# Four graph layers on one core: a reordered softmax, first pairs one step sooner, a bias add in pieces, and a normalisation moved to ScalarE

## Chip, cores and metric

The kernel runs on one core of a Trainium2 chip. Five engines share the core's on-chip memory: PE (TensorE, matrix products), ACT (ScalarE), DVE (VectorE), POOL (GpSimd) and SP (SyncE, which here issues the transfers). The metric is the device time of one execution in microseconds (us), as the median of several runs. Smaller is better.

## What is computed

`x` holds 32 batches of 512 nodes with 128 features, `adj` is a sparse 512 x 512 matrix. Four layers follow each other, each of the form x = x + layer(relu(layernorm(x))). Cut to what matters:

```python
h = relu(layernorm(x))                       # layer 0
A = softmax(where(adj > 0, e[position], -9e15), axis=1)
x = x + (A*I) @ (h @ W0) + (A*(1-I)) @ (h @ W1) + bias

h = relu(layernorm(x))                       # layer 1
x1 = adj^T h;  x2 = 2*adj^T x1 - h
x = x + relu(concat(h, x1, x2, x1, x2) @ Theta1 + bias)

h = relu(layernorm(x))                       # layer 2
f = relu(h @ psi_w + psi_b);  msg = (adj*adj)^T f
x = x + relu(concat(msg, h) @ phi1_w + phi1_b) @ phi2_w + phi2_b

h = relu(layernorm(x))                       # layer 3
S = exp(8*tanh(((h@q) @ (h@k)^T) / sqrt(128) / 8)) * adj
x = x + (S / rowsum(S)) @ h @ v
```

All is in float32. Inputs and output lie in the chip's main memory.

## The kernel before

**Tiling.** The 32 batches are worked on as 16 pairs, q = 0 to 15. A pair's `x` is one tile of 128 partitions x 2 batches x 4 blocks of 128 nodes x 128 features. All 16 pairs stay on chip through the four layers, so `adj` and what is derived from it are made once.

**Names.** `bn` are the layer norm's statistics (L194, VectorE), `sd` the roots (L200, ScalarE), `rs` and `sh` the scale and shift (L203, L205, VectorE). `h` is the normalised tile. It is made by eight ScalarE instructions of 128x128 (L216), which apply scale, shift and relu at once. In layer 3 alone it is made by eight VectorE instructions (L229) and two relus on ScalarE (L231). `hT` is h with features on the partitions. For the pairs 0, 1 and 2 of layer 0 it is made by transposes on the PE and two copies on ScalarE (L248, L251). For the others it goes through VectorE's 32x32 transposes (`hb`, L258) and a bounce through main memory (L262, L265).

**Prep (up to L614).** Inside the `by_source` block the PE, VectorE, ScalarE and GpSimd run in the order of the source. The block builds the softmax matrix `att` from `adj`, with the exponentials in `softmax_rows` (L550) and the division in `scaled_rows` (L560). `transpose_rows` (L400) makes `attT`. The chebyshev matrix `cheb` is made in four pieces (L409), each of four matmuls of 512 columns, an eviction and a correction of the diagonal. The layer norm of pairs 0 and 1 runs between these, as the generators `normal`, `turned` (hT) and `project` (the product with W1, called `g`).

**Matrix products.** Products of a 512 x 512 matrix with a pair are formed from seven half-size products (`products`, L299, in the order of `ORDER`, L296). They need sums of the matrix's quarters (`sum_steps`) and of the pair's (`right_blocks`, `rt`, on GpSimd). Each product's bank is emptied by one instruction: in `mixed` (L323) by ScalarE for two of them and by VectorE for the rest. The banks are named a, c and d (`p_msgT_a` and so on), and c and a are used again by later products.

**The layers.** `layer0(q)` does the seven products with `att`, adds the diagonal part and ends with the statistics for layer 1. `layer1(q)` makes x1T and x2T, and then p_l (L706), y (L709) and the new x (L710). `layer2(q)` makes `feat` (L721 to L724), msgT, adds the bias phi2b to x on GpSimd as one instruction (L730), and then makes h1T (L737) and x (L741). `layer3(q)` makes, for each batch of the pair, p_qkh and p_hv, then four score blocks with tanh and exp (L765 to L770), and then p_av (L777), the division, the add to x and the output transfer (L784).

**Order.** After the prep, generators are called in turn. `waiting` is a list of groups of generators. In every step the next group joins `active`, and each active generator advances by one `yield`. This gives the order in which instructions are emitted. A scheduler then orders each engine's instructions, with the exception of those marked `keep_in_program_order`, and every engine runs its own queue. `layer0_first(q)` makes h, hT and g of a later pair, so that layer 0 finds them ready; `loads(q)` starts the transfers of later pairs; `square()` and `late_sums()` prepare the matrices of later layers.

```python
waiting = [[layer0(q)] for q in range(NQ)]          # L806
for q in range(2, NQ):
    waiting[max(q - 4, 0)].append(first[q])
waiting += [[layer1(q)] for q in range(NQ)]
```

Of the kernel before, what the change touches and what calls it, by code (L numbers as in the profile page):

```python
# [11 lines left out]
AF = mybir.ActivationFunctionType  # L12
# [3 lines left out]
P = 128  # L16
# [8 lines left out]
def kernel(  # L25
# [98 lines left out]
    def spread(w, n):  # L124
        return w[:, None, :].to_broadcast([P, n, D])
# [86 lines left out]
    def normed_steps(q, h):  # L212
        for b in range(2):
            for t in range(NT):
                i = b * NT + t
                nc.scalar.activation(h[:, b, t, :], xt[q][:, b, t, :], AF.Relu,  # L216
                                     bias=shift[q][:, i : i + 1], scale=scale[q][:, i : i + 1])
                yield

    def normed(q, on_act=True):  # L220
        h = normed_tile(q)
        if on_act:
            for _ in normed_steps(q, h):
                pass
            return h
        for b in range(2):
            for t in range(NT):
                i = b * NT + t
                nc.vector.tensor_scalar(h[:, b, t, :], xt[q][:, b, t, :], scale[q][:, i : i + 1],  # L229
                                        shift[q][:, i : i + 1], OP.mult, OP.add)  # L230
            nc.scalar.activation(h[:, b], h[:, b], AF.Relu)  # L231
        return h


# [165 lines left out]
    def transpose_rows(banks, src, t):  # L400

        for j in range(NT):
            nc.tensor.transpose(banks[j][:, blk(t)], src[:, t, blk(j)], ident)
# [156 lines left out]
    def scaled_rows(t, u):  # L560
        nc.vector.reciprocal(total[:, t : t + 1], total[:, t : t + 1])
        nc.scalar.mul(split(att[:, t, :]), crossed(u), total[:, t : t + 1])
        own = split(att[:, t, :])[:, :, t, :]
        d = diag[:, t, :].rearrange("p (b c) -> p b c", c=QR)
        nc.gpsimd.tensor_mul(d, own, ident.rearrange("p (b c) -> p b c", c=QR))
        nc.gpsimd.tensor_sub(own, own, d)
# [8 lines left out]
    pt = [bank(f"p_attT_{j}") for j in range(NT)]  # L575
    us = []
    for t in range(NT):
        if t == NT - 1:
            next(project[0], None)
        us.append(softmax_rows(t))  # L580
        if t == 0:
            next(ln[1], None)
        else:
            scaled_rows(t - 1, us[t - 1])
        for _ in range(3):
            next(normal[1], None)
    scaled_rows(NT - 1, us[-1])
    next(turned[1])
    for t in range(NT):
        transpose_rows(pt, att, t)  # L590
    next(turned[1], None)
    nc.scalar.copy(qk, p[:, :D])
    rights = {0: right_of(0)}
    next(project[1])
    for q in (2, 3):
        next(ln[q])
    for j in range(NT):
        (nc.vector.tensor_copy if j % 2 else nc.scalar.copy)(attT[:, j, :], pt[j])
    next(project[1], None)
    for _ in sum_steps(attT, "att", nc.vector):  # L600
        pass
# [6 lines left out]
    for q in (2, 3):  # L608
        next(ln[q])
        next(ln[q], None)  # L610
    for i in (2, 3):
        for _ in pieces[i]:
            pass
    by_source.__exit__(None, None, None)  # L614


# [96 lines left out]
    def layer2(q):  # L713
        h = normed(q)
        yield
        hT = transposed(h, f"hT2_{q}")
        yield
        yield
        feat = []
        for b in range(2):  # L720
            pf = projected(f"p_feat_{q}_{b}", (at(hT, b), psi))  # L721
            feat.append(late.tile([P, NT, D], F32, tag="y", name=f"feat_{q}_{b}", bufs=2))
            nc.vector.tensor_add(feat[b], pf, spread(psib, NT))
            nc.scalar.activation(feat[b], feat[b], AF.Relu)  # L724
        yield
        right = right_blocks(lambda J, b: feat[b][:, 2 * J : 2 * J + 2, :], f"feat_{q}", [nc.gpsimd] * 4)
        msgT = pair_tile(f"msgT_{q}").rearrange("p (b w) -> p b w", b=2)
        for _ in mixed(f"msgT_{q}", sums["sq"], right, msgT):
            pass
        nc.gpsimd.tensor_add(xt[q], xt[q], phi2b[:, None, None, :].to_broadcast([P, 2, NT, D]))  # L730
        yield
        h1T = pair_tile(f"h1T_{q}").rearrange("p (b w) -> p b w", b=2)
        for b in range(2):
            ph = bank(f"p_phi1_{q}_{b}")
            nc.tensor.matmul(ph, phi1[:, 1, :], hT[:, :, b, :], start=True, stop=False)
            nc.tensor.matmul(ph, phi1[:, 0, :], msgT[:, b], start=False, stop=True)  # L736
            nc.scalar.activation(crossed(h1T[:, b]), split(ph), AF.Relu, bias=phi1b)  # L737
        yield
        for b in range(2):
            po = projected(f"p_l2_{q}_{b}", (columns(h1T[:, b]), phi2))  # L740
            nc.vector.tensor_add(xt[q][:, b], po, xt[q][:, b])  # L741
        ln_stats(q)

    def layer3(q):
        h = normed(q, on_act=False)
        yield
        hT = transposed(h, f"hT3_{q}")
        yield
        yield
        for b in range(2):  # L750
            pp = bank(f"p_qkh_{q}_{b}")
            nc.tensor.matmul(pp, qk, hT[:, :, b, :], start=True, stop=True)  # L752
            both = work.tile([P, 2 * N + 2 * NT], F32, tag="pair", name=f"qkh_hv_{q}_{b}", bufs=5)
            qkh = both[:, :N]
            nc.vector.tensor_copy(crossed(qkh), split(pp))

            pv = projected(f"p_hv_{q}_{b}", (at(hT, b), vw))
            hv = both[:, N : N + NT * (D + 1)].rearrange("p (t f) -> p t f", f=D + 1)
            nc.gpsimd.memset(hv[:, :, D : D + 1], 1.0)
            nc.vector.tensor_copy(hv[:, :, :D], pv)  # L760
            yield
            ex = square_tile(f"ex_{q}_{b}")
            for t in range(NT):
                ps = bank(f"p_score_{q}_{b}_{t}")
                nc.tensor.matmul(ps, hT[:, t, b, :], qkh, start=True, stop=True)  # L765
                nc.scalar.activation(ex[:, t, :], ps, AF.Tanh, scale=1.0 / (8.0 * math.sqrt(D)))  # L766
            for t in range(NT):
                nc.scalar.activation(ex[:, t, :], ex[:, t, :], AF.Exp, scale=8.0)  # L768
                eng = nc.gpsimd if t % 2 else nc.vector
                eng.tensor_mul(ex[:, t, :], ex[:, t, :], adjTx[0][:, t, :])  # L770
            yield
            rsum = stats.tile([P, NT], F32, tag="rsum", name=f"rsum_{q}_{b}", bufs=4)
            for i0 in range(0, NT, 2):
                po = bank(f"p_av_{q}_{b}_{i0}").rearrange("p (i f) -> p i f", i=2)
                for i in range(2):
                    for t in range(NT):
                        nc.tensor.matmul(po[:, i, : D + 1], ex[:, t, blk(i0 + i)], hv[:, t, :],  # L777
                                         start=(t == 0), stop=(t == NT - 1))
                nc.vector.reciprocal(rsum[:, i0 : i0 + 2], po[:, :, D])
                for i in range(2):  # L780
                    xi = xt[q][:, b, i0 + i, :]
                    nc.vector.scalar_tensor_tensor(xi, po[:, i, :D], rsum[:, i0 + i : i0 + i + 1], xi,
                                                   OP.mult, OP.add)
            nc.sync.dma_start(out[2 * q + b].rearrange("(t p) f -> p t f", p=P), xt[q][:, b])  # L784

    adjTx = []

    def square():

        sq = square_tile("sq")  # L790
        load_crossed(sq, adj)
        adjTx.append(square_tile("adjTx"))
        load_crossed(adjTx[0], adjT_d)
        yield
        for i in range(NT):
            s = late.tile([P, N], F32, tag="hs", name=f"sq_{i}", bufs=2)
# [8 lines left out]

    waiting = [[layer0(q)] for q in range(NQ)]  # L806
    next(waiting[0][0])
    for q in range(NQ // 2, NQ):
        waiting[q - NQ // 2].append(loads(q))
    for q in range(2, NQ):  # L810
        waiting[max(q - 4, 0)].append(first[q])
    waiting[3].append(late_sums())
    waiting += [[layer1(q)] for q in range(NQ)]
    waiting[NQ + 6].append(square())
    for layer in (layer2, layer3):
        waiting += [[layer(q)] for q in range(NQ)]
    active = []
    while waiting or active:
        if waiting:
            active += waiting.pop(0)  # L820
        active = [g for g in active if next(g, active) is not active]


# [30 lines left out]
```

## Time and profile before

| what | value |
|---|---|
| median of 3 runs | 998.58 us (997.66 to 998.66) |
| the profiled execution's own time | 1000.32 us |
| its span, first to last instruction | 998.5 us |
| mean granted PE clock | 0.993 |
| last matmul ends | 994.34 us |
| instructions | 16127 |

In the profile a line such as `L216 ACT ... x384 | 154.5, 482` means: the instruction of line 216 ran 384 times on ScalarE, 154.5 us in all, 482 ns each. After the next bar stands the idle time of the engine just before these instructions, and what ended it. A timeline gives start, duration, engine, line, operation, output and inputs; idle time before an instruction stands in brackets with what released it. The stages can be told from the lines that run: the prep up to about 49 us, layer 0 to about 201, layer 1 to about 487, layer 2 to about 717, and layer 3 to the end.

### The profile page before, as it was taken

How to read it: one execution, taken by the hardware profiler on the slowest of the kernel's cores; microseconds unless marked ns; L12 is line 12 of the kernel's file. 1: busy time of each engine (PE TensorE's matmuls, PEld its weight loads, DVE VectorE, ACT ScalarE, POOL GpSimd, SP SyncE). 2: the span in 40 equal slices, each digit the busy share in tenths (PEclk: the TensorE clock that was granted, in tenths of full speed). 3: DMA queues.
4: the chain of work that ended last, by engine and by line, in shares of the span. 5: the costliest groups of instructions: out<-in, count | busy, mean ns of one | idle time of the engine just before them, and what ended most of it. 6: DMA issues, size and time to landing. Idle time of an engine off the chain costs nothing.

```text
span 998.5 us, 16127 instructions
## 1 busy us (share of the span) xinstructions
PE 976.4 (98%) x5918; PEld 809.4 (81%) x5918; DVE 630.4 (63%) x1520; ACT 440.9 (44%) x967; POOL 395.1 (40%) x478
## 2 busy tenths in 40 slices
PE   8999999999999999999899999999999999999997
PEld 4699999989999999998777777777667777767776
DVE  8678787655555655558667888777754444444443
ACT  4863537112322323237566343333464455544452
POOL 2579998841217213136455112222132333222332
PEclk9999999999999999999899999999999999999999
DMA  9256644412131222215333344322222121211111
GB/s 254 85 134 179 179 125 130 106 52 76 43 85 43 64 64 54 73 44 140 93 94 106 102 121 122 90 71 78 69 70 74 43 74 53 72 55 54 53 30 35
DMA packets 83007, 87.17 MB, mean 87 GB/s; under 512 B 6768, under 2 KB 73072, under 8 KB 82928
## 3 DMA queue, kind: packets, MB, share of 16 engines
q1 hardware_dynamic: 82928, 86.14, 30.7%
q8 instruction: 47, 0.77, 0.3%
q14 instruction: 32, 0.26, 0.1%
HBM read 44.70 MB, written 41.42 MB: 86 GB/s over the span
## 4 chain that ended last, share of the span: by engine, by line
PE 88%; DVE 6%; ACT 2%; DMA 1%; issue 1%; POOL 1%; SPq 1%; POOLq 0%; DVEq 0%; ACTq 0%
PE p_av L777 11%; PE p_score L765 10%; PE p_l L365 10%; PE p_msgT_c L312 4%; PE p_l_c L319 4%; PE p_x1T_c L312 4%; PE p_x2T_c L312 4%; PE p_hv L365 3%; PE p_g L365 3%; PE p_msgT_a L312 3%; PE p_x1T_a L312 3%; PE p_x1T_d L312 3%; PE p_x2T_a L312 3%; PE p_x2T_d L312 3%; PE p_qkh L752 3%; PE p_l_d L319 3%
## 5 line engine op out<-in xcount | busy, mean ns | idle before, releaser
L216 ACT ACTIVATE h<-x,sh,rs 128x128 f32<-128x128 f32 x384 | 154.5, 482 | 58.4 <-PE p_x2T_d L312 46.0
L770 POOL TENSOR_TENSOR ex<-ex,adjTx 128x512 f32<-128x512 f32 x64 | 83.3, 1303 | 200.3 <-issue 147.7
L777 PEld LDWEIGHTS p_av<-qkh_hv,ex 128*128 128x128 f32 x1024 | 120.3, 193 | 11.6 <-issue 6.9
L766 ACT ACTIVATE ex<-p_score 128x512 f32<-128x512 f32 x128 | 71.8, 587 | 130.6 <-issue 112.9
L777 PE MATMUL p_av<-qkh_hv,ex 128*128 128x129 f32 x1024 | 122.9, 277 | 2.2 <-POOL ex L770 1.4
L765 PE MATMUL p_score<-qkh_hv,hT 128*128 128x512 f32 x256 | 115.1, 592 | 0.0
L258 DVE STREAM_TRANSPOSE hb_hT<-h 128x512 f32<-128x512 f32 x122 | 84.8, 701 | 24.5 <-ACT h L216 23.9
L194 DVE BATCH_NORM_STATS2 bn<-x 128x6 f32<-128x256 f32 x256 | 95.1, 419 | 1.9
L770 DVE TENSOR_TENSOR ex<-ex,adjTx 128x512 f32<-128x512 f32 x64 | 45.9, 717 | 76.1 <-ACT ex L768 76.1
L765 PEld LDWEIGHTS p_score<-qkh_hv,hT 128*128 128x128 f32 x256 | 46.2, 190 | 46.4 <-issue 44.2
L768 ACT ACTIVATE ex<-ex 128x512 f32<-128x512 f32 x128 | 76.5, 630 | 1.9
L290 POOL TENSOR_TENSOR rt_h<-h 128x256 f32<-128x256 f32 x16 | 11.6, 727 | 133.9 <-PE p_x2T_c L312 133.1
L290 POOL TENSOR_TENSOR rt_feat<-feat,feat 128x256 f32<-128x256 f32 x16 | 11.6, 726 | 126.3 <-ACT feat L724 126.3
L730 POOL TENSOR_TENSOR x<-x,phi2b 128x1024 f32<-128x1024 f32 x16 | 38.0, 2375 | 33.2 <-ACT h L216 33.2
L365 PE MATMUL p_l<-th,x2T 128*128 128x128 f32 x256 | 49.5, 275 | 0.0
L365 PE MATMUL p_l<-th,x1T 128*128 128x128 f32 x256 | 49.5, 275 | 0.0
L365 PE MATMUL p_l<-th,hs 128*128 128x128 f32 x256 | 49.5, 275 | 0.0
L397 ACT COPY g<-p_g 128x512 f32<-128x512 f32 x32 | 18.3, 579 | 62.4 <-PE p_g L365 62.3
L365 PEld LDWEIGHTS p_hv<-vw,hT 128*128 128x128 f32 x256 | 33.6, 192 | 14.9 <-issue 7.9
L634 POOL TENSOR_TENSOR hd<-hT,adiag 128x512 f32<-128x512 f32 x32 | 40.3, 1273 | 7.1 <-PE p_l_e L655 2.5
L737 ACT ACTIVATE h1T<-p_phi,phi1b 128x512 f32<-128x512 f32 x32 | 21.9, 686 | 44.9 <-PE p_phi L736 44.9
L365 PEld LDWEIGHTS p_l<-th,hs 128*128 128x128 f32 x256 | 40.1, 192 | 0.8
(229 smaller groups left out, 2181.0 us busy)
## 6 DMA issues: line engine op xcount, KB each, us to landing
d_hT<-hb_hT SPq DMA_DIRECT2D x244, 128.0 KB
hT<-d_hT SPq DMA_DIRECT2D x61, 512.0 KB
x<-in_x_dram SPq DMA_DIRECT2D x32, 256.0 KB
out_dram<-x SPq DMA_DIRECT2D x32, 256.0 KB
adj_s<-in_adj_dram SPq DMA_DIRECT2D x4, 256.0 KB
adjT_d<-adjT SPq DMA_DIRECT2D x1, 1024.0 KB
sq<-in_adj_dram SPq DMA_DIRECT2D x4, 256.0 KB
adjTx<-adjT_d SPq DMA_DIRECT2D x4, 256.0 KB
```

Source lines behind the costliest of these rows:

```text
L194: ins = nc.vector.bn_stats(st[:, k].rearrange("p e s -> p (e s)"), xt[q][:, b, t : t + 2, :].rearrange("p t f -> p f t"))
L216: nc.scalar.activation(h[:, b, t, :], xt[q][:, b, t, :], AF.Relu, bias=shift[q][:, i : i + 1], scale=scale[q][:, i : i + 1])
L258: nc.vector.transpose(hb[:, :, b].rearrange("p j t r -> p t j r"), h[:, b].rearrange("p t (j c) -> p t j c", c=QR))
L312: nc.tensor.matmul(p[:, :H], b[:, k, :], a[:, k, :], start=(first and k == 0), stop=(k == 1), skip_group_check=True)
L319: nc.tensor.matmul(p[:, i * D : (i + 1) * D], a[:, k, blk(i)], b[:, k, :], start=(first and i == 0 and k == 0), stop=(k == 1), skip_group_ ...
L365: nc.tensor.matmul(p[:, blk(t)], hT(t), w, start=(i == 0), stop=(i == len(terms) - 1))
L634: nc.gpsimd.tensor_mul(split(s), src, split(scale))
L765: nc.tensor.matmul(ps, hT[:, t, b, :], qkh, start=True, stop=True)
L766: nc.scalar.activation(ex[:, t, :], ps, AF.Tanh, scale=1.0 / (8.0 * math.sqrt(D)))
L768: nc.scalar.activation(ex[:, t, :], ex[:, t, :], AF.Exp, scale=8.0)
L770: eng.tensor_mul(ex[:, t, :], ex[:, t, :], adjTx[0][:, t, :])
L777: nc.tensor.matmul(po[:, i, : D + 1], ex[:, t, blk(i0 + i)], hv[:, t, :], start=(t == 0), stop=(t == NT - 1))
```

## The change

The diff has six parts.

1. In the prep, the copies of pair 0's g (the second step of `project[0]`) move from before the last softmax row to after it, two rather than three steps of pair 1's normalisation go with each row, the transposes of att's first two row blocks and chebyshev piece 2 are emitted at row 2, and pair 1's transposes and copies follow those of att.
2. In layer 2, the phi2b add of 128x1024 becomes four adds of 128x256, kept in program order.
3. Layer 3's normalisation uses the same eight ScalarE instructions as the other layers.
4. Layer 1's and layer 2's pair 0 join one step sooner, ahead of the last pair of the layer before; `square()` moves with them.
5. Pairs 2 and 3 of layer 0 are advanced before the loop: pair 2 is normalised, pair 3 normalised and transposed. Pairs 2 and 4 join in the first step, 3 and 5 in the second.
6. When only two generators are left, their order is reversed, and the last output transfer is issued in two halves.

```diff
 softmax and transposes
     for t in range(NT):
-        if t == NT - 1:
-            next(project[0], None)
         us.append(softmax_rows(t))
...
-        for _ in range(3):
-            next(normal[1], None)
+        if t < NT - 1:
+            for _ in range(2):
+                next(normal[1])
+        if t == 2:
+            transpose_rows(pt, att, 0)
+            transpose_rows(pt, att, 1)
+            next(pieces[2])
+            next(pieces[2])
     scaled_rows(NT - 1, us[-1])
+    next(project[0], None)
+    for _ in normal[1]:
+        pass
+    transpose_rows(pt, att, 2)
+    transpose_rows(pt, att, 3)
     next(turned[1])
-    for t in range(NT):
-        transpose_rows(pt, att, t)
-    next(turned[1], None)
-    nc.scalar.copy(qk, p[:, :D])
     rights = {0: right_of(0)}
-    next(project[1])
     for q in (2, 3):
         next(ln[q])
     for j in range(NT):
         (nc.vector.tensor_copy if j % 2 else nc.scalar.copy)(attT[:, j, :], pt[j])
+    next(turned[1], None)
+    next(project[1])
+    nc.scalar.copy(qk, p[:, :D])
+    next(pieces[2], None)
     next(project[1], None)
...
-    for i in (2, 3):
-        for _ in pieces[i]:
-            pass
+    for _ in pieces[3]:
+        pass
 layer2
-        nc.gpsimd.tensor_add(xt[q], xt[q], phi2b[:, None, None, :].to_broadcast([P, 2, NT, D]))
+        for b in range(2):
+            for i in range(0, NT, 2):
+                xi = xt[q][:, b, i : i + 2, :]
+                tc.keep_in_program_order(nc.gpsimd.tensor_add(xi, xi, spread(phi2b, 2)))
 layer3
-        h = normed(q, on_act=False)
+        h = normed(q)
...
+                if b == 1 and q == NQ - 1:
+                    nc.sync.dma_start(out_r[:, i0 : i0 + 2, :], xt[q][:, b, i0 : i0 + 2, :])
+            if not (b == 1 and q == NQ - 1):
+                nc.sync.dma_start(out_r, xt[q][:, b])
 the loop
     next(waiting[0][0])
+    next(first[2])
+    next(first[3])
+    next(first[3])
...
-    for q in range(2, NQ):
-        waiting[max(q - 4, 0)].append(first[q])
+    waiting[0] += [first[2], first[4]]
+    waiting[1] += [first[3], first[5]]
+    for q in range(6, NQ):
+        waiting[q - 4].append(first[q])
     waiting[3].append(late_sums())
-    waiting += [[layer1(q)] for q in range(NQ)]
-    waiting[NQ + 6].append(square())
-    for layer in (layer2, layer3):
-        waiting += [[layer(q)] for q in range(NQ)]
+    waiting[-1].insert(0, layer1(0))
+    waiting += [[layer1(q)] for q in range(1, NQ)]
+    waiting[NQ + 5].append(square())
+    waiting[-1].insert(0, layer2(0))
+    waiting += [[layer2(q)] for q in range(1, NQ)]
+    waiting += [[layer3(q)] for q in range(NQ)]
     active = []
     while waiting or active:
         if waiting:
             active += waiting.pop(0)
+        if not waiting and len(active) == 2:
+            active.reverse()
```

More of the change, by code (lines that the diff above doesn't have):

```diff
@@ L218, in normed_steps, with normed @@
                 yield
-    def normed(q, on_act=True):
+    def normed(q):
         h = normed_tile(q)
-        if on_act:
-            for _ in normed_steps(q, h):
-                pass
-            return h
-        for b in range(2):
-            for t in range(NT):
[L228 to L231, printed above, removed]
+        for _ in normed_steps(q, h):
+            pass
         return h
@@ L584 @@
             scaled_rows(t - 1, us[t - 1])
-        for _ in range(3):
-            next(normal[1], None)
-    scaled_rows(NT - 1, us[-1])
+        if t < NT - 1:
[6 more added lines that the diff above has]
+            next(pieces[2])
+    scaled_rows(NT - 1, us[-1])
+    next(project[0], None)
[3 more added lines that the diff above has]
+    transpose_rows(pt, att, 3)
     next(turned[1])
-    for t in range(NT):
-        transpose_rows(pt, att, t)
-    next(turned[1], None)
-    nc.scalar.copy(qk, p[:, :D])
     rights = {0: right_of(0)}
-    next(project[1])
     for q in (2, 3):
@@ L610 @@
         next(ln[q], None)
-    for i in (2, 3):
-        for _ in pieces[i]:
-            pass
+    for _ in pieces[3]:
+        pass
     by_source.__exit__(None, None, None)
@@ L771, in layer3 @@
             yield
+            out_r = out[2 * q + b].rearrange("(t p) f -> p t f", p=P)
             rsum = stats.tile([P, NT], F32, tag="rsum", name=f"rsum_{q}_{b}", bufs=4)
@@ L783, in layer3 @@
                                                    OP.mult, OP.add)
-            nc.sync.dma_start(out[2 * q + b].rearrange("(t p) f -> p t f", p=P), xt[q][:, b])
+                if b == 1 and q == NQ - 1:
+                    nc.sync.dma_start(out_r[:, i0 : i0 + 2, :], xt[q][:, b, i0 : i0 + 2, :])
+            if not (b == 1 and q == NQ - 1):
+                nc.sync.dma_start(out_r, xt[q][:, b])
     adjTx = []
```

## The prediction

> **What bounds the kernel now.** I read the page's engine sums, then the waits of the PE (TensorE), then the PE's own timeline around each wait, and last ScalarE, VectorE and GpSimd at those places. The sums come first:
>
> ```profile
> PE 976.4 (98%) x5918; PEld 809.4 (81%) x5918; DVE 630.4 (63%) x1520; ACT 440.9 (44%) x967; POOL 395.1 (40%) x478
> ```
>
> The PE is busy for 976.4 of 998.5 us and no other engine passes 63%. The change removes no matmul. So only three things can move: PE idle time, PE time at half clock, and the tail after the last matmul (994.34 to 998.5). The list of the PE's waits says where the idle time is; its columns are total, times, longest:
>
> ```profile
> PE p_msgT_a L312 <- ACT feat L724: 3.5, 1, 3.5
> PE p_attT L403 <- ACT hT L251: 2.1, 1, 2.1
> PE p_x1T_c L312 <- DVE u_x1T L332: 1.8, 1, 1.8
> PE p_msgT_c L312 <- DVE u_msgT L332: 1.5, 2, 1.3
> PE p_l_c L319 <- DVE u_l L667: 1.4, 3, 0.8
> PE p_av L777 <- POOL ex L770: 1.4, 2, 0.9
> ```
>
> They are single events, each at the border of two stages. In the timeline they stand at 34.44 (p_attT), 457.80 (p_x1T_c), 493.08 (p_msgT_a), 551.50 and 565.07 (p_msgT_c), 988.24 and 990.20 (p_av). The half clock is the second cost, seen in the view of stretches (PEclk is the number after the engines):
>
> ```profile
> 491.00:493.00 2.00, 0.00 (x0) 0.00 (x0) 2.00 (x5) 0.61 (x1) 0.21 (x1) 0.84 0.00 0
> 493.00:499.00 6.00, 5.46 (x12) 3.94 (x13) 1.97 (x6) 3.38 (x10) 2.81 (x4) 0.50 0.37 88
> ```
>
> The clock records put it at 38.38-41.79, 492.35-499.18 and 990.70-994.11, each time following a stall of the list. What makes the longest stall is on VectorE:
>
> ```profile
> 485.14 0.69 DVE L709 TENSOR_TENSOR y<-p_l,b 128x512 f32<-128x512 f32 x1 [1.04 <-PE p_l L365]
> 485.86 2.83 DVE L710 SCALAR_TENSOR_TENSOR x<-y,x 128x512 f32<-128x512 f32 x1
> ...
> 490.11 1.65 DVE L710 SCALAR_TENSOR_TENSOR x<-y,x 128x512 f32<-128x512 f32 x1
> 491.68 0.68 DVE L723 TENSOR_TENSOR feat<-p_feat,psib 128x512 f32<-128x512 f32 x1
> ```
>
> The same instruction has a median of 0.691 us over 32. The slow ones lie beside the one-piece phi2 bias on GpSimd:
>
> ```profile
> L730 POOL TENSOR_TENSOR x<-x,phi2b 128x1024 f32<-128x1024 f32 x16 | 38.0, 2375 | 33.2 <-ACT h L216 33.2
> ```
>
> **What the Trainium skill says.** "SBUF — State Buffer", on who interferes with whom: VectorE and GpSimd share a port pair that one holds exclusively for a whole instruction. The trace agrees: 2.83 for 0.69 us there, and the first L229 beside L730 takes 1.35 us (median 0.342). "TensorE: Matmul & The Clock Gate", Part 1: an idle window of some 3.4 us halves the clock and a busy window restores it. Here the half-clock stretches are 3.41 and 6.83 us. "Perfetto Trace Analysis", Tensor Engine Instruction: ScalarE, VectorE and GpSimd run strictly in order; this carries the stall I add below.
>
> **Part by part** (minus is gained).
>
> 1. Softmax reordered. The g_0 copies (L397, 1.04 us at 33.05) leave ScalarE ahead of the last exp (34.00), so the last att row is ready about 1.0 sooner, 36.4. The PE fills its 2.10 us hole with chebyshev piece 2 (8 matmuls x 0.429 = 3.43 us), which before came after. Then the last two attT transposes run, then hT_1's, then a wait of about 0.9, because the hT_1 copies (0.53 each) now stand behind attT's. p_g_1 starts at 39.9 rather than 37.98 but with 3.43 us more work behind it: -1.5. The half clock at 38.38 goes: 16 p_g took 3.25 us, against 1.79 warm, and p_adiag slowed too: -1.6. Sum **-3.1**; layer0(0) starts about 46.05 for 49.16.
>
> 2. First pairs turned ahead of the loop: a new stall. Pair 2's p_hT is followed on the PE by p_g_2, which waits for two hT copies (L251). Before, ScalarE had been idle 5.80 us when they came:
>
> ```profile
> 58.32 1.07 ACT L251 COPY hT<-p_hT 128x512 f32<-128x512 f32 x2 [5.80 <-PE p_hT L248]
> 58.96 0.71 PE L365 MATMUL p_g<-w,hT 128*128 128x128 f32 x4 [0.24 <-ACT hT L251]
> ```
>
> In the changed program's order on ScalarE they stand behind sd_0, sd_4, the eight h_4 and sd_5. Those wait for VectorE's statistics, which need layer 0's last add. With p_l_e ending at 57.85 - 3.1 = 54.75: add 0.41, four bn 1.4, sd and rs and sh with the bn of pairs 4 and 5 between, some 1.8, so h_4 starts near 58.35; eight h at a spacing of 0.397 (row L216 has 482 ns each, overlapping) 3.17; sd_5 0.25; copy 0.53: p_g_2 at about 62.4, where 58.96 - 3.1 = 55.86 was to be had. 6.55 us lost; PE idle about 6.7. That is two windows' length, so half clock follows for 3.4 to 6.8 us, in which half the work is lost beyond its warm time: 2.15 (1.4 to 2.9). Sum **+8.7**; with part 1 layer 0 is +5.6. No row shows this wait: from below, if the copies are reached at once, 0; from above, if the statistics of pair 5 come first in full, 10. I take 8.7, since the order on ScalarE is fixed. The stall at 200.94 (0.81) is not touched.
>
> 3. phi2 bias in four pieces of 128x256 (0.72 each by the rt_h row's 727 ns), held in program order. They no longer run beside layer 1's end. The wait at 457.80 came from an L710 of 2.30 us ahead of u_x1T: **-1.8**. In layer 2 the two p_msgT_c waits go likewise (1.29 and 0.26, after an L229 of 1.35): **-1.55**. A stretched VectorE instruction now costs at most about 0.73, not 2.36.
>
> 4. First pairs of layers 1 and 2 a step sooner. p_feat_0 comes before p_l_15, whose 24 matmuls x 0.22 = 5.36 us cover the chain. Feat adds done at 485.4, relus 486.2, four rt_feat at 0.73 until 489.2, when p_msgT_a is due: the 3.51 wait and 0.46 behind it go, -3.97, and the half clock, 5.64 us of PE work at double time, -2.8. Sum **-6.8**. If the chain is 1 us late, it costs 1 us and no half clock. Layer 1's first pair begins behind work that keeps the PE busy either way: 0.
>
> 5. Last layer normalised on ScalarE. VectorE loses 128 tensor_scalar (37.0 us), ScalarE trades 32 relus (20.2) for 128 h x 0.40 (51). Both have room on average; the order matters. From the sixth step of layer 2 two h stand ahead of the second h1T and one ahead of the u_msgT copy on ScalarE; they wait for sh on VectorE, which a bias piece can hold for 0.35 on average. In the steady step at 664-684 the PE has that little slack: 0.2 x 8 steps, **+1.5** (0 to 4). At the border of layers 2 and 3 the last h's push the first tanh and exp by 1.35, most under p_score and p_av: **+0.4** (0 to 1.5). DMA queues keep the same transfers; the hT3 bounces start under a microsecond later with more than a step of lead.
>
> 6. Tail. With the last two generators reversed, the last p_score is issued before the p_av of the pair's other half, so 3.58 us of p_av hide the exps and multiplies that now show as 0.93 and 0.42, with the half clock behind them (p_av at half rate until 994.11). Last matmul 994.34 to about 990.35: **-4.0**. The last output transfer is 128 KB for 256: **-0.3** (0 to 0.8).
>
> Sum: -3.1 + 8.7 - 1.8 - 1.55 - 6.8 + 1.5 + 0.4 - 4.0 - 0.3 = -6.95. The profiled execution took 1000.32 (span 998.5 and 1.8 around it), so 993.4 there; the runs' median is 998.58, 1.7 lower, so **991.7**. Its own range is 988.5 to 995.5.
>
> **Rivals.** (a) The pair 2 stall is not there: the h_4 are ready early or the PE has other work. For it: ScalarE is only 44% busy and idle before those copies now. Against it: its fixed order. It gives 991.7 - 8.7 = 983.0; 10%. (b) Layer 1 to 2 keeps its stall, because feat's chain, moved forward, meets VectorE just as busy with L709, L710 and bn (485 to 491.6 in the lines above). Against it: without the one-piece bias these shrink from 5.9 to 2.8 us. It gives 991.7 + 6.8 = 998.5; 7%. (c) Slower: in layer 2 the bias pieces lock VectorE's sh and rs, the h behind them hold h1T and u_msgT on ScalarE in every step, and the PE waits. For it: sh took 0.70 for 0.17 beside rt_feat at 548.59. One piece (0.73) and part of a second make 0.9 to 1.3 us for each of 14 steps, in place of my 1.5 in all: 1002.8 to 1008.4. It decides from 0.6 us a step (8.4 us, the sum and its 1.5). Against it: a step lasts some 14 us (493 to 717 for 16 pairs), with other gaps for four pieces; 8%.
>
> **Numbers.** Forecast 75%, (a) 10%, (b) 7%, (c) 8%. The range reaches down to (a) and up to where half of (b) begins: 983 to 997. A measurement of this kernel tells 0.2% (2.0 us) from no change: faster is below 996.6, slower above 1000.6. The forecast gives 73 faster and 2 the same, (a) 10 faster, (b) 3 faster and 4 the same, (c) 1 the same and 7 slower: 86, 7, 7.
>
> **What would show it.** Right: p_attT without its 2.1 wait and clock 1.0 from 25 to 50; a wait of 6 to 7 us of p_g on hT (L251) near 55 to 62 with half clock behind; no L710 over 1.5 us; p_msgT_a without wait, clock 1.0 at 485 to 500; last matmul some 4 us after the last p_score's multiplies and no half clock. Wrong: p_g_2 within 1 us of its transposes (then a); p_msgT_a waiting over 2 us (b); waits of p_phi or p_msgT_c on ScalarE in many steps of layer 2 (c).

## The result, and the profile after

| | before | changed |
|---|---|---|
| median | 998.12 us (997.25 to 998.66, 4 runs) | 990.31 us (990.08 to 991.01, 4 runs) |
| profiled execution's own time | 1000.32 us | 990.44 us |
| its span | 998.5 us | 988.6 us |
| last matmul ends | 994.34 us | 984.88 us |

The ratio is 0.9924, with a 95% interval of 0.9907 to 0.9941. The kernel became 7.8 us faster by the medians; 991.7 was forecast. Between the two profiled executions the difference is larger, 9.9 us. The profiled execution of before was about 2 us above its own median, and what follows shows one place where such a difference comes from.

The page's engine sums of the changed kernel:

```profile
PE 970.4 (98%) x5918; PEld 805.4 (81%) x5918; DVE 590.4 (60%) x1392; ACT 469.3 (47%) x1063; POOL 399.3 (40%) x526
```

The PE still sets the time, with the same 5918 matmuls and 6.0 us less busy time; no matmul is gone, so their records are shorter. The half clock accounts for some 3.5 us of it: by the clock records, the PE worked for 12.5 us at half before and for 5.4 us now. The rest stays open. Part 3 alone (e11 below) takes 35 of the 40 us that VectorE is less busy, and brings ScalarE's 28 us more. The list of the PE's waits in the changed kernel (columns: total, times, longest):

```profile
PE p_g L357 <- ACT hT L243: 6.6, 2, 6.1
PE p_msgT_c L304 <- POOL rt_feat L283: 1.4, 1, 1.4
PE p_l_c L311 <- DVE u_l L666: 1.2, 2, 0.8
PE p_av L780 <- POOL qkh_hv L761: 0.6, 1, 0.6
PE p_attT L395 <- POOL att L558: 0.3, 1, 0.3
PE p_av L780 <- POOL ex L772: 0.2, 1, 0.2
```

The waits of p_msgT_a (3.5), p_attT on hT (2.1), p_x1T_c (1.8), p_msgT_c on u_msgT (1.5) and p_av on ex (1.4) are gone or small. Two are new: p_g on hT, 6.1 us, as forecast, and p_msgT_c on rt_feat, 1.4 us, which was not. The view of stretches of the changed kernel (PEclk is the third number from the end):

```profile
25.00:50.00 25.00, 24.29 (x138) 17.01 (x137) 16.45 (x39) 20.98 (x48) 14.33 (x23) 1.00 0.23 85
59.00:66.00 7.00, 5.22 (x24) 5.22 (x25) 2.65 (x6) 6.31 (x16) 1.33 (x2) 0.52 0.81 230
492.00:499.00 7.00, 7.00 (x40) 6.18 (x39) 3.94 (x9) 3.96 (x11) 2.40 (x4) 1.00 0.02 6
975.00:985.00 10.00, 9.88 (x71) 8.25 (x69) 3.72 (x12) 4.35 (x8) 2.54 (x2) 1.00 0.11 33
```

The half clock has moved: it is gone from 25 to 50, from layer 2's start and from the end, and it stands behind the new wait, where the clock records give 6.83 us from 59.33. ScalarE's timeline there, in the changed kernel:

```profile
55.23 0.30 ACT L200 ACTIVATE sd<-bn,eps 128x8 f32<-128x8 f32 x1 [3.40 <-DVE bn L194]
55.89 0.30 ACT L200 ACTIVATE sd<-bn,eps 128x8 f32<-128x8 f32 x1 [0.35 <-DVE bn L194]
56.88 3.19 ACT L216 ACTIVATE h<-x,sh,rs 128x128 f32<-128x128 f32 x8 [0.68 <-DVE sh L205]
59.98 0.29 ACT L200 ACTIVATE sd<-bn,eps 128x8 f32<-128x8 f32 x1
60.17 1.04 ACT L243 COPY hT<-p_hT 128x512 f32<-128x512 f32 x2
```

The data of the two copies lay ready from 54.68, when the transposes ended. ScalarE, idle at that time, waited for sd_0, which stands ahead of them in its queue, then for sd_4, and then ran the eight h of pair 4 and sd_5. The copies came at 60.17. The view of L709 (L710 before) shows that no instance is stretched any more; its numbers are shortest, median and longest in ns:

```profile
L709 DVE SCALAR_TENSOR_TENSOR x<-y,x x32: 647/650/693, 227.0 to 498.9; 128x512 f32<-128x512 f32 x32
```

Set side by side, the start of the same matmul in both traces gives where the time went. A minus is gained:

| stretch, bounded by the start of a matmul (the last two rows by the last matmul's end and the end of the span) | forecast | measured |
|---|---|---|
| prep and layer 0's first pair (to p_l_e of pair 0) | -3.1 | -4.0 |
| pair 2's p_g (from there to pair 4's p_g) | +8.7 | +8.4 |
| layer 1's end (to pair 15's p_x1T_a) | -1.8 | -2.1 |
| layer 1 to 2 (to pair 2's p_msgT_a) | -6.8 | -5.8 |
| layer 2, pairs 2 to 8 | -1.55 | -2.75 |
| layer 2, pairs 8 to 15 (to pair 15's p_phi) | +1.5 | +0.3 |
| layer 2 to 3 | +0.4 | +0.1 |
| the last pair | -4.0 | -3.7 |
| after the last matmul | -0.3 | -0.4 |
| sum | -6.95 | -9.9 |

The sizes are near. Whether the parts of the change are what I took them for is another question, and the experiments answer it differently in three places.

### The profile page after: what moved, and what is told of

Its sections match the earlier page's. It is cut to its first block, busy times and chain, and to the rows that moved or that the text cites. A ratio compares the mean times of both kernels' runs of the same rounds, so it can differ in the third digit from the quotient of the medians.

```text
span 988.6 us, 16123 instructions
## 1 busy us (share of the span) xinstructions
PE 970.4 (98%) x5918; PEld 805.4 (81%) x5918; DVE 590.4 (60%) x1392; ACT 469.3 (47%) x1063; POOL 399.3 (40%) x526
## 4 chain that ended last, share of the span: by engine, by line
PE 91%; ACT 1%; DVE 1%; POOL 1%; issue 0%; DVEq 0%; ACTq 0%
PE p_av L780 12%; PE p_l L357 11%; PE p_score L767 11%; PE p_msgT_c L304 4%; PE p_x2T_c L304 4%; PE p_x1T_c L304 4%; PE p_l_c L311 4%; PE p_feat L357 3%; PE p_msgT_d L304 3%; PE p_x1T_a L304 3%; PE p_hv L357 3%; PE p_x2T_d L304 3%; PE p_x2T_a L304 3%; PE p_x1T_d L304 3%; PE p_msgT_a L304 3%; PE p_qkh L754 3%
## 5 line engine op out<-in xcount | busy, mean ns | idle before, releaser
L216 ACT ACTIVATE h<-x,sh,rs 128x128 f32<-128x128 f32 x512 | 208.7, 483 | 70.3 <-PE p_x2T_d L304 46.5
L780 PE MATMUL p_av<-qkh_hv,ex 128*128 128x129 f32 x1024 | 120.3, 275 | 0.9 <-POOL qkh_hv L761 0.6
L732 POOL TENSOR_TENSOR x<-x,phi2b 128x256 f32<-128x256 f32 x64 | 44.4, 726 | 0.0
L631 POOL COPY hs<-hT 128x512 f32<-128x512 f32 x32 | 19.6, 611 | 54.7 <-PE p_l L357 40.5
L330 ACT COPY x1T<-p_x1T_a 128x256 f32<-128x256 f32 x16 | 6.0, 372 | 74.8 <-PE p_x1T_a L304 74.8
```

The costliest lines, as they stand in the source:

```text
L732: tc.keep_in_program_order(nc.gpsimd.tensor_add(xi, xi, spread(phi2b, 2)))
```

## The experiments

Each is compared with runs of the kernel before on the same chip; the medians of before lay between 998.12 and 999.31. "w/o" stands for the changed kernel with one part undone.

| kernel | median us | ratio to before, 95% interval |
|---|---|---|
| changed | 990.31 | 0.9924 [0.9907, 0.9941] |
| e1, w/o part 5 | 985.73 | 0.9866 [0.9848, 0.9884] |
| e2, changed, copies held ahead | 982.90 | 0.9840 [0.9822, 0.9858] |
| e3, w/o part 4 | 992.12 | 0.9931 [0.9916, 0.9947] |
| e4, w/o part 2 | 992.12 | 0.9934 [0.9918, 0.9951] |
| e5, w/o part 3 | 1007.21 | 1.0090 [1.0074, 1.0106] |
| e6, w/o the reversal of part 6 | 992.78 | 0.9944 [0.9927, 0.9960] |
| e7, w/o part 1 | 990.71 | 0.9920 [0.9904, 0.9936] |
| e8, e2 and the bias after h | 982.24 | 0.9836 [0.9819, 0.9854] |
| e9, e2 w/o part 1 | 986.62 | 0.9879 [0.9863, 0.9895] |
| e10, before and part 2 alone | 1007.74 | 1.0087 [1.0072, 1.0102] |
| e11, before and part 3 alone | 992.72 | 0.9941 [0.9928, 0.9954] |
| e12, e8 and late statistics | 978.88 | 0.9801 [0.9787, 0.9814] |

**e1: part 5 undone.**

```diff
-    next(first[2])
-    next(first[3])
-    next(first[3])
...
-    waiting[0] += [first[2], first[4]]
-    waiting[1] += [first[3], first[5]]
-    for q in range(6, NQ):
-        waiting[q - 4].append(first[q])
+    for q in range(2, NQ):
+        waiting[max(q - 4, 0)].append(first[q])
```

> The changed kernel with part 5 undone: pairs 2 to 4 join in the first step as before, nothing of them is advanced ahead of the loop. On ScalarE the two hT copies of pair 2 then stand right behind h_3, ahead of sd_0, sd_4 and h_4. My theory (the 6.1 us wait of p_g on hT at 54.68 and the half clock behind it come from the copies' place on ScalarE): the wait falls under 0.5 us, no half clock at 59 to 66, and the span shrinks by 8.4 us (the step from -4.04 to +4.38 between the two profiles): median about 982. Rival (part 5 pays for itself: without it pair 3's transposes and bounce come late and the PE waits for p_g_3 or hT instead): the wait moves to the next pair and the time stays within 2 us of 990.3.

985.73 us: faster than the changed kernel, so part 5 as it stands costs 4.6 us, but less than the 8.4 expected. The list of the PE's waits of e1:

```profile
PE p_l_c L311 <- DVE u_l L666: 2.5, 3, 1.3
PE p_g L357 <- DMA hT<-d_hT: 1.6, 1, 1.6
```

The wait of p_g on ScalarE's copies fell to two of 0.7 us together, without half clock. The rival is right for the rest: pair 3's hT now comes late from its bounce (1.6 us at 66.09), and a wait of 1.3 us of p_l_c, at 81.92, is new. Part 5 does something useful and something harmful, and the two can be parted.

**e2: all parts, the copies held ahead of h_4.** The two copies of pair 2, the h of pair 4 and the sd of pairs 4 and 5 are kept in the order of the source on ScalarE:

```diff
-            nc.scalar.copy(hT[:, :, b, :].rearrange("p b (a c) -> p b a c", c=QR), crossed(p))
+            ins = nc.scalar.copy(hT[:, :, b, :].rearrange("p b (a c) -> p b a c", c=QR), crossed(p))
+            if name == "hT0_2":
+                tc.keep_in_program_order(ins)
...
+                if q == 4 and len(early) < 4:
+                    tc.keep_in_program_order(ins)
...
+        if q in (4, 5) and len(early) < 4:
+            tc.keep_in_program_order(ins)
```

> The changed kernel with all its parts, but on ScalarE the two hT copies of pair 2 are held ahead of sd_4, h_4 and sd_5; sd_0 stays ahead of them. Theory (place on ScalarE alone): the wait of p_g on hT falls from 6.1 to about 1.5 us (sd_0 ends at 55.5, then one copy of 0.53), no half clock follows, time about 990.3 - 4.6 - 2.2 = 983.5. Rival (pair 2's wait is due to the earlier pairs' statistics on VectorE as such, or h_4 held back makes pair 4 late): the time stays above 987.

982.90 us, near the 983.5 expected. ScalarE's timeline in e2, at the place shown above:

```profile
55.55 0.30 ACT L200 ACTIVATE sd<-bn,eps 128x8 f32<-128x8 f32 x1 [3.41 <-DVE bn L194]
55.76 1.05 ACT L247 COPY hT<-p_hT 128x512 f32<-128x512 f32 x2
56.70 0.31 ACT L200 ACTIVATE sd<-bn,eps 128x8 f32<-128x8 f32 x1
```

The copies run at 55.76 rather than 60.17, p_g_2 waits 1.4 us rather than 6.1, and no half clock stands in the records after that. In the later pairs of layer 0, e2's p_l_a start 6.8 to 6.95 us ahead of those of the changed kernel. The distance is still 6.9 us at the last matmul, so all of it arises here: the place of two copies in one queue was worth 7.4 us of the median. In the source they come ahead of h_4; the scheduler had put them behind.

**e3 and e4: part 4 undone, part 2 undone.** In e3 the loop's lists for layers 1 and 2 are those of before; in e4 the bias is one instruction of 128x1024 again, which the scheduler may move.

```diff
 e3
-    waiting[-1].insert(0, layer1(0))
-    waiting += [[layer1(q)] for q in range(1, NQ)]
-    waiting[NQ + 5].append(square())
-    waiting[-1].insert(0, layer2(0))
-    waiting += [[layer2(q)] for q in range(1, NQ)]
-    waiting += [[layer3(q)] for q in range(NQ)]
+    waiting += [[layer1(q)] for q in range(NQ)]
+    waiting[NQ + 6].append(square())
+    for layer in (layer2, layer3):
+        waiting += [[layer(q)] for q in range(NQ)]
 e4
-        for b in range(2):
-            for i in range(0, NT, 2):
-                xi = xt[q][:, b, i : i + 2, :]
-                tc.keep_in_program_order(nc.gpsimd.tensor_add(xi, xi, spread(phi2b, 2)))
+        nc.gpsimd.tensor_add(xt[q], xt[q], phi2b[:, None, None, :].to_broadcast([P, 2, NT, D]))
```

> The changed kernel with part 4 undone: the first pairs of layers 1 and 2 start one step later, as before; the bias stays in four pieces. If part 4 is what removed the 3.51 us wait of p_msgT_a, as I reckoned: it comes back with its half clock, time about 990.3 + 6.8 = 997. If the bias in pieces already removed most of it, since L710 no longer stretches to 2.83 us: p_msgT_a waits 1 to 2 us, no half clock, time about 991 to 992.5. Between the two: both are needed.

> The changed kernel with the phi2 bias back as one instruction of 128x1024 on GpSimd (2.36 us). My theory: L710 of layer 1's last pair stretches again to over 2 us and p_x1T_c waits about 1.8 us, and the p_msgT_c waits in layer 2 come back (1.55 us), time about 990.3 + 3.4 = 993.7; if the early feat chain meets the stretched L710 too, up to 6 us more with half clock. Rival (with part 4 the scheduler puts the bias elsewhere, so that the pieces are not what removed the waits): within 1 us of 990.3.

Each costs 1.8 us of the median, where I had 6.8 for part 4 alone. The PE's waits of e3 at the border of layers 1 and 2:

```profile
PE p_msgT_a L304 <- ACT feat L723: 1.0, 1, 1.0
PE p_msgT_c L304 <- POOL rt_feat L283: 0.7, 1, 0.7
PE p_msgT_a L304 <- ACT u_msgT L322: 0.5, 1, 0.5
```

The pieces alone cut the 3.51 us wait to 0.98, since L709 is no longer stretched (693 ns at most), and no half clock follows there. The waits of e4, and its L709:

```profile
PE p_x1T_c L304 <- DVE u_x1T L324: 1.8, 1, 1.8
PE p_msgT_c L304 <- POOL rt_feat L283: 1.7, 1, 1.7
PE p_msgT_a L304 <- ACT feat L723: 0.2, 1, 0.2
L709 DVE SCALAR_TENSOR_TENSOR x<-y,x x32: 649/691/2328, 226.6 to 502.3; 128x512 f32<-128x512 f32 x32
```

Part 4 alone cuts it to 0.2, though L709 is as long as 2328 ns again. So either part removes the long stall and its half clock; the gain of 6.8 us belongs to neither alone. The 1.8 us of p_x1T_c are back in e4, as expected. The two p_msgT_c waits on u_msgT are not, although the bias is in one piece again: what removed those was not part 2. Nor are the pieces all gain there: from pair 4 to pair 15 a step of layer 2 takes 13.05 us in e4, and 13.28 from pair 7 on in the changed kernel.

**e5: part 3 undone.** Layer 3 is normalised by VectorE (L229) and two relus, as before; the bias stays in pieces. The branch of `normed` that does it is back too, and is left out here.

```diff
-        h = normed(q)
+        h = normed(q, on_act=False)
```

> The changed kernel with part 3 undone: layer 3's h made by eight tensor_scalar on VectorE and two relus on ScalarE; the bias stays in four pieces. My reckoning was that the pieces remove the two p_msgT_c waits in the middle of layer 2 (1.55 us) and that the eight h on ScalarE cost 1.5 us in its second half: then this runs 1.5 to 2 us faster than the changed kernel, about 988.5. Rival (part 3 removed those waits, since the stretched instruction there was the L229 on VectorE; the run with the bias in one piece kept them away too): the waits come back and the time is 1 to 3 us more, about 991.5 to 993.

1007.21 us, slower than before. The rival has the direction, and neither had the size. The PE's waits in e5:

```profile
PE p_msgT_c L312 <- DVE u_msgT L332: 7.7, 12, 1.6
PE p_msgT_a L312 <- ACT u_msgT L330: 5.4, 8, 0.7
```

And one of these steps in e5's timeline, GpSimd, VectorE, ScalarE and the PE together:

```profile
660.73 1.41 POOL L740 TENSOR_TENSOR x<-x,phi2b 128x256 f32<-128x256 f32 x2
660.78 2.73 DVE L229 TENSOR_SCALAR h<-x,rs,sh 128x128 f32<-128x128 f32 x7
...
662.52 0.63 ACT L231 ACTIVATE h<-h 128x512 f32<-128x512 f32 x1 [1.60 <-DVE h L229]
663.06 0.35 ACT L330 COPY u_msgT<-p_msgT_a 128x256 f32<-128x256 f32 x1
...
663.47 0.70 PE L312 MATMUL p_msgT_a<-sq,feat 128*128 128x256 f32 x2 [0.68 <-ACT u_msgT L330]
...
664.50 1.13 PE L312 MATMUL p_msgT_c<-sq,rt_feat 128*128 128x256 f32 x4 [0.33 <-DVE u_msgT L332]
```

Read downwards: the pieces run beside the L229, the relu on ScalarE waits for them for 1.60 us, the copy of u_msgT stands behind the relu in the same queue, and p_msgT_a and p_msgT_c wait for it. No single L229 is stretched beyond 840 ns (the median of this run is 336), but for each of layer 3's pairs 5 to 13 three of the eight take 0.7 us or more. The eight of pairs 7 to 13 take 3.36 us, for 2.14 in the kernel before, and a step of layer 2 takes 14.8 us for 13.3. From pair 4 of layer 2 to pair 15's p_phi, e5 loses 15.8 us against before. The bias in one piece had not done this to the kernel before, and its place tells why. GpSimd's last two L730 in the profile of before:

```profile
538.24 2.37 POOL L730 TENSOR_TENSOR x<-x,phi2b 128x1024 f32<-128x1024 f32 x1 [4.46 <-ACT h L216]
546.22 2.36 POOL L730 TENSOR_TENSOR x<-x,phi2b 128x1024 f32<-128x1024 f32 x1
```

All 16 are done by 548.6, because the scheduler could move them ahead. Held in program order, the pieces lie in every step up to the end of layer 2, beside whatever else is there.

**e6: the reversal undone.** The last transfer stays in two halves.

```diff
-        if not waiting and len(active) == 2:
-            active.reverse()
```

> The changed kernel without the reversal of the last two generators; the last transfer stays in two halves. Theory (the last p_score ahead of the other half's p_av hides the exps and multiplies): p_av waits 1.3 us in two places behind ex on GpSimd and half clock follows to the end; the last matmul ends 3.7 us later, median about 994. Rival (the gain at the end came from the last layer's h on ScalarE, which leaves VectorE free for the multiplies): within 1 us of 990.3.

992.78 us. From the first p_qkh of the last pair's second batch to the last matmul's end, e6 takes 16.4 us for the changed kernel's 12.7: 3.7 us, as expected, with the 0.93 and 0.42 us and the half clock back. The ratios differ by 0.0020, about 2 us, so the runs show less than the two traces do; the intervals overlap. The traces of e10 and e11 (below), which have the old order here, point to why. They have the same waits of 0.93 and 0.42 us, but no half clock behind them before the last matmul, and the same stretch takes 14.8 us. So the order is worth 2.0 us, and 1.6 more in an execution in which the half clock follows. The rival falls: e5, without part 3, takes 12.7 us there like the changed kernel. The PE's waits in e6, and then the stretch around the same waits in e10 (PEclk 1.00):

```profile
PE p_av L780 <- POOL ex L772: 1.5, 3, 0.9
```

```profile
PE p_av L780 <- POOL ex L773: 1.4, 2, 0.9
990.00:1001.70 11.70, 10.24 (x62) 7.53 (x61) 3.72 (x11) 4.35 (x8) 2.53 (x2) 1.00 0.08 24
```

**e7: the prep in its old order.** The diff of the softmax part shown with the change, reversed.

> The changed kernel with the prep in its old order (part 1 undone). Theory: p_attT waits about 2 us for the hT copies again, half clock follows, and p_l_e of pair 0 ends 4.0 us later (57.6 for 53.5); the later wait of p_g on hT stays: median about 994.3. Rival (what part 1 gains is taken back at the wait of p_g on hT, since h_4 hangs on statistics that were not made sooner): that wait shrinks by 2 us or more and the time is under 992.5.

990.71 us for 990.31: part 1 moves nothing that can be measured. The rival is right. In e7's trace p_attT waits 2.1 us again, and pair 0's p_l_e starts 3.0 us later than in the changed kernel, but pair 2's p_g starts only 0.45 us later (61.23 for 60.78). ScalarE's timeline in e7:

```profile
58.07 0.50 ACT L200 ACTIVATE sd<-bn,eps 128x8 f32<-128x8 f32 x2 [6.56 <-DVE bn L194]
59.45 1.26 ACT L216 ACTIVATE h<-x,sh,rs 128x128 f32<-128x128 f32 x3 [0.87 <-DVE sh L205]
60.61 1.04 ACT L243 COPY hT<-p_hT 128x512 f32<-128x512 f32 x2
```

Here three h stand ahead of the copies, and no sd_5, because the scheduler placed them otherwise. The wait of p_g is 3.52 rather than 6.11 us. Part 1 made the first pair ready 3.0 us sooner and gave 2.6 back at the same queue.

**e9: e2 without part 1.** The same reversal in e2, to see whether that was all.

> The kernel with pair 2's hT copies held ahead of h_4 (982.9), with the prep in its old order. Theory (part 1 gains 3 us up to layer 0's first pair, and the run without it, 990.7, showed only 0.4 because the wait of p_g on hT took it back): with that wait gone, leaving part 1 out costs 2.5 to 3.5 us, about 986. Rival (part 1's gain is taken back by something else in layer 0): within 1 us of 982.9.

986.62 us for 982.90, so part 1 is worth 3.7 us (2.8 between the two traces) once the queue no longer takes it back. The theory holds.

**e10 and e11: one part alone, in the kernel before.** In e10 the bias becomes four pieces, in e11 layer 3's h goes to ScalarE.

```diff
 e10
-        nc.gpsimd.tensor_add(xt[q], xt[q], phi2b[:, None, None, :].to_broadcast([P, 2, NT, D]))
+        for b in range(2):
+            for i in range(0, NT, 2):
+                xi = xt[q][:, b, i : i + 2, :]
+                tc.keep_in_program_order(nc.gpsimd.tensor_add(xi, xi, spread(phi2b, 2)))
 e11
-        h = normed(q, on_act=False)
+        h = normed(q)
```

> The kernel before with the bias in four pieces and nothing else. If the pieces are bad beside a normalisation on VectorE whatever else is done (the run without part 3 lost 15.8 us in layer 2): it gains some 6.3 us up to layer 2's first steps (L710 no longer stretched) and loses 15.8 after, about 1008. Rival (that loss needs the other parts, the first pairs a step sooner or the changed order): under 998.

> The kernel before with layer 3's normalisation on ScalarE and nothing else. Theory (the two p_msgT_c waits in layer 2 and the 0.24 us of each later step come from the normalisation on VectorE, not from the bias being in one piece): layer 2 loses nothing after its fourth step, as in the run with the bias in one piece (4.3 us), about 994. Rival (my reckoning: h on ScalarE costs 1.5 us and gains nothing without the pieces): 998 to 1000.

1007.74 and 992.72 us: both theories hold. By the traces, e10 is 6.9 us ahead of before at pair 4 of layer 2, and 9.0 behind at its end. Its longest wait is that of e5:

```profile
PE p_msgT_c L312 <- DVE u_msgT L332: 10.2, 12, 1.6
```

Part 2 alone makes the kernel slower by 0.9%; part 3 alone makes it faster by 0.6%. In e11 the waits of p_msgT_c on u_msgT are gone and layer 2 gains 4.2 us from pair 4 on. So the victim that mattered was the L229 on VectorE. Part 2 does two things, it cuts the instruction and holds the pieces in order; four pieces that the scheduler may move, or one piece held, were not tried.

**e8 and e12: further on from e2.** In e8 the four adds, put into a function `bias_pieces`, are emitted for pairs 4 to 15 right after the pair's h, for which they then wait. In e12, in addition, pair 15's statistics for layer 2 are made at the start of its own step.

```diff
 e8
     def layer2(q):
         h = normed(q)
+        if q >= 4:
+            bias_pieces(q)
...
+        if q < 4:
+            bias_pieces(q)
 e12, layer1
-        ln_stats(q)
+        if q < NQ - 1:
+            ln_stats(q)
 e12, layer2
+        if q == NQ - 1:
+            ln_stats(q, hold=True)
         h = normed(q)
```

> The kernel with the hT copies of pair 2 held ahead of h_4 (982.9 before), and for pairs 4 to 15 the four bias pieces emitted right after the pair's h, on which they then wait, so that they start after sh and no longer lie beside it. Theory (in the second half of layer 2 each step loses 0.24 us because a piece holds VectorE's sh at 0.45 for 0.15 us, h and the u_msgT copy follow late on ScalarE, and p_msgT_c waits): the steps from pair 8 to 15 take 13.05 rather than 13.28 us, time about 981.2. Rival (the pieces now stretch VectorE's u_msgT adds or the transposes): same 982.9 or up to 2 us more.

> The kernel with the copies held and the bias after h (982.2), and the statistics of pair 15 made at the start of its layer 2 step rather than at the end of layer 1, so that four bn no longer stand ahead of pair 1's two feat adds on VectorE. Theory (the 1.41 us wait of p_msgT_c on rt_feat comes from these): the wait falls to 0.2 to 0.5 us, time about 981. Rival (the bn come later at a worse place, or the wait hangs on p_feat and the relus): 982 or more.

e8 took 982.24 us, which the runs don't tell from e2's 982.90. Its trace shows what was meant in part. In the last three steps of layer 2, VectorE's sh is no longer held by a piece; it ran as follows in the changed kernel, and then in e8:

```profile
662.24 0.45 DVE L205 SCALAR_TENSOR_TENSOR sh<-bn,rs 128x8 f32<-128x8 f32 x1
```

```profile
653.96 0.17 DVE L207 SCALAR_TENSOR_TENSOR sh<-bn,rs 128x8 f32<-128x8 f32 x1
```

These three steps take 13.05 us each. But the steps of pairs 7 to 11 still lose about 0.23 us each, at p_msgT_c, and ahead of each of them a piece still lies beside sh, which takes 0.44 to 0.68 us. Ahead of pair 10's step in e8:

```profile
614.34 0.45 DVE L207 SCALAR_TENSOR_TENSOR sh<-bn,rs 128x8 f32<-128x8 f32 x1
```

e12 took 978.88 us (978.70 to 978.96), below the 981 expected. All that is left of the PE's waits from layer 0 on:

```profile
PE p_g L363 <- ACT hT L247: 1.9, 2, 1.4
PE p_l_c L317 <- DVE u_l L672: 1.3, 2, 0.8
PE p_av L795 <- POOL qkh_hv L776: 0.6, 1, 0.6
```

The 1.4 us wait on rt_feat is gone, so it did come from four bn ahead of two feat adds. By the traces this gives 1.6 us. Another 0.9 us comes between pairs 8 and 12 of layer 2, where the steps take 13.05 us again. Ahead of the steps of pairs 8 to 10 sh still takes 0.44 us, but the order on ScalarE is another: the h now stand behind the copy of u_msgT, not ahead of it. In these traces, then, the held sh costs only where h that need it stand ahead of that copy. e12 is the fastest kernel here, 2.0% under before.

## Why the prediction was right, and where its steps were not

The time was right: 991.7 was forecast, 990.31 measured, with the direction and the range. The main view, that only single waits of the PE, its half clock and the tail can move, held in every run.

- **Part 2 of the prediction's list (pairs turned ahead): right, mechanism and size.** A wait of about 6.7 us was forecast and 6.11 measured; p_g_2 at 62.4, measured at 60.78; +8.7 in all, measured +8.4. e2 shows that the queue's order is the cause. Rival (a), that there is no such stall, falls.
- **Part 1 of the list (softmax): the term as such was near (-3.1, measured -4.0), the independence was not.** I added the terms of parts 1 and 2 as if they stood alone. e7 and e9 show that part 1 is worth 0.4 us with the stall and 3.7 without it.
- **"First pairs of layers 1 and 2 a step sooner: -6.8": right as a sum, wrong in what it was given to.** e3 and e4 show that the pieces remove most of the same stall. Rival (b), that p_msgT_a keeps its wait, falls: it has none in the changed kernel. The step also missed the next wait: pair 1's rt_feat, 1.41 us late, because the four bn of pair 15 stand ahead of the feat adds on VectorE (e12).
- **The pieces "no longer run beside layer 1's end", -1.8: right.** The 1.8 us wait is there in e4 and e11, which have the bias in one piece, and in no kernel with the pieces; -2.1 measured.
- **"In layer 2 the two p_msgT_c waits go likewise", by the pieces: wrong.** This is the step that failed. I called all the waits border events, but these two stand at 551.50 and 565.07, inside layer 2, where L229 begins. I took the stretched L229 for a matter of how long one bias instruction is, with "at most about 0.73" for one of them. One takes no more than 0.84 us in e5, but three in a row are held in each step. e5 and e10 show that with the pieces these waits become more, 12 of up to 1.6 us, and e11 that taking L229 away from VectorE is what removes them. The error hid in the sum because both parts were in the change; that it did so is luck.
- **"h on ScalarE: +1.5 in the second half of layer 2": the mechanism is there, the comparison was not.** The changed kernel does lose 0.24 us a step from pair 7 on because a piece holds sh and the h behind it stand ahead of u_msgT. Where one of the two is missing (the last three steps of e8, e12, and e4 with its single piece) the loss is gone. But the kernel before lost as much there, by another way: pairs 10 and 11 together took 26.58 us before and 26.57 after, and 26.10 in e11, which has neither the pieces nor the L229 in these steps. Net it was +0.3.
- **Rival (c), the slower one: a mechanism of its kind exists, and its price came true in other kernels.** I put 0.9 to 1.3 us a step on the pieces' hold of VectorE with ScalarE's queue behind it, 1002.8 to 1008.4 in all. e10 and e5 lose some 1.5 us a step, though through the held L229 and its relu rather than through sh, rs and h on ScalarE, and took 1007.74 and 1007.21 us. It was not decided by the size of the pieces but by whether VectorE still makes the h.
- **Tail: right between the traces, less in the runs.** -4.0 and -0.3 forecast, -3.7 and -0.4 measured between the traces. Of the 3.7, 1.6 hang on a half clock that does not follow in every execution (e10, e11). The split of the last transfer was not tried apart.
- **The sum** was 3 us short of the traces' difference, but the trace of before is of an execution 2 us above its median. I carried the sum over to the median unchanged, and the median moved by 7.8, not 9.9. So it is partly luck that the forecast lies only 1.4 us from the median: what the sum lacked and what that one execution had too much nearly cancel.

## What to carry to other kernels

Undo each part of a change that has several: here one part was harmful alone (+0.9%) and gained 1.8 us beside another, and one was worth 0.4 us until a third was mended and 3.7 after. Where an engine runs its queue in order, look at what stands ahead of a short instruction that the bottleneck waits for: two copies behind another pair's statistics cost 7 us. And an instruction held in program order is not only cut or pinned but moved: look at where it ran before, and what runs beside it now.

## What the runs showed of the hardware

The same PE wait was followed by half clocks of different length. The kernel before and e11 both waited 3.51 us for p_msgT_a. The clock records then show 6.83 us at half in the one and 3.41 us in the other, and from p_feat to the next pair's p_msgT_a e11 was 1.0 us shorter for it. The view of stretches of before, and then of e11, from 493 to 500 us:

```profile
493.00:500.00 7.00, 6.46 (x16) 4.67 (x17) 2.40 (x7) 4.38 (x13) 2.81 (x4) 0.56 0.32 77
```

```profile
493.00:500.00 7.00, 6.09 (x19) 4.45 (x20) 2.77 (x8) 5.23 (x13) 2.90 (x5) 0.76 0.37 77
```

The 2.10 us wait of p_attT was followed by 3.41 us at half in before, e10 and e11, and by none in e7 and e9, which have the same order there. The waits of 0.93 and 0.42 us of the last p_av were followed by 3.41 us in before and e6, and by none ahead of the last matmul in e10 and e11.

The length of a record is not yet its price, since it can begin during the wait, when there is nothing to slow down. At the 6.1 us wait of p_g the records show 6.83 us at half in the changed kernel, e3, e4 and e5, and 10.24 in e6. In e6 some 4 us of it lie within the wait. What lies behind the wait is 3.2 us in e5, 5.4 in the changed kernel and 6.1 in e6, and from pair 2's p_g to pair 4's these took 21.3, 22.3 and 22.6 us, for 19.8 in e2, where no half clock stands.

The Trainium skill, "TensorE: Matmul & The Clock Gate", Part 1, says that the clock is decided in windows of about 3.4 us that run on their own; records in multiples of 3.41 us and these differences agree with it. The idle window of that length, on which the prediction leaned, does not: half clock followed waits of 2.10 us, and of 0.93 and 0.42, in some of the traces. Here the measurement decides, and what else it takes no run shows. So the price of what follows a stall is not one number, and one profiled execution can hold a dear or a cheap case. The runs of before agree: those of 995.4 us show a mean granted clock of 0.998, those of 1000.4 us and more 0.993 or 0.994. The stalls themselves (2.10, 3.51 and 6.1 us) repeat to some hundredths of a us.
